# The end of a two-layer graph network: one row tile's root moved to GpSimd, four tiles' roots in one batch, and the last stores grouped otherwise

## The chip, the cores and the metric

The kernel runs on one core of one Trainium2 chip. The core has TensorE for matmuls, VectorE (DVE in the profile), ScalarE (ACT) and GpSimd (POOL) for everything elementwise, SyncE (SP), which here only issues DMAs, and 16 DMA engines. The metric is the time of one execution in microseconds (us) on the device, as the median of several runs.

## The reference

Sixteen graphs of 1024 nodes with 256 features each, and a 0/1 adjacency matrix for each. Two layers follow one another; each adds a message to the features and normalises every row.

```python
def _layernorm(x, axis=-1, eps=1e-5):
    m = jnp.mean(x, axis=axis, keepdims=True)
    v = jnp.var(x, axis=axis, keepdims=True)
    return (x - m) / jnp.sqrt(v + eps)

# layer 0: e0 = leaky(einsum('bid,bjd->bij', h * a0, h)); a0..a3 belong to adj == 1..4
alpha = sigmoid(where(adj == 1, e0, -max))          # adj is 0 or 1 in the data
x = _layernorm(x + einsum('bij,bjd->bid', alpha, h) + bias)

# layer 1
Hh = einsum('bni,io->bno', h, W)
s, d = Hh @ a_src, Hh @ a_dst
e = where(adj != 0, exp(-leaky_relu(s[:, :, None] + d[:, None, :], 0.2)), 0)
x = _layernorm(x + elu(einsum('bnm,bmo->bno', e, Hh) / rowsum(e)))
```

All the change happens in the last line, for the last graph: the quotient, the elu (which is `max(v, 0) + min(exp(v), 1) - 1`), the sum with the features, and the normalisation of each row, which needs the row's mean and the reciprocal root of its variance.

## The kernel before, in words

The main path (`one_kind_pass`) assumes that the adjacency holds only zeros and ones and checks that on the way; at the very end each engine reads a flag (`n_bad`), and a slow general path (`general_pass`) runs if the assumption failed. It does not fail on these data, so the timed execution takes the other branch, which holds only the last store (`y_last`).

The graphs go through in a software pipeline: while graph `b` is in layer 0, graph `b - 1` is in layer 1, and graph `b - 2` gets its last scalings and stores. A row tile is 128 nodes; a graph has eight. The order of all work is written out by hand: each engine works through its own instructions in the order in which the program issues them, and waits for others through semaphores. An instruction that waits holds up everything behind it on the same engine.

The last graph (`last`, index 15) has no next graph to run beside. Its layer 1 ends the kernel, and only this end is changed:

- TensorE sums tiles 0 to 3 together (`first`), then tiles 4, 5 and 6 one by one (`multiply1`), then tile 7 (`end`) in two halves of columns (`multiply_halves`): first columns 128 to 255 with the row sum, then columns 0 to 127. Each sum lies in a PSUM accumulator `acc`.
- For each tile, `elu` (lines 684 to 694) takes the reciprocal of the row sum on VectorE (`rinv`), then the relu and the exponential of the scaled sum on ScalarE (`h`, L693, and `y`, L694). For tile 6, VectorE makes `h` (L690, L691).
- `add` (L699, L706) joins them on VectorE, and `stats` (L326, L328) takes the mean and variance of the rows: `bn_stats` into `st`, then `bn_aggr` into `mv`. For tile 6 the aggregation is left for later.
- `center` turns the variances of a batch of tiles into `r` (the reciprocal root) and `mr` (minus mean times `r`) on GpSimd: L336 adds epsilon, L357 raises to the power of -0.5, L360 to L363 refine that by a Newton step, L373 and L374 make `mr`. Before the change it is called for tiles 0 to 2 at `t == 4`, and for tiles 3 to 5 at `t == 5`.
- `scale1` (L379) applies `r` and `mr` to a tile on ScalarE; `store` (L721) sends tiles out, from SP's queue or, with `nc.scalar`, from ScalarE's.
- At `t == 5` each engine reads the flag (L1064): ScalarE, SP and VectorE on their way, GpSimd behind its batch of roots. ScalarE then scales the last two tiles of graph 14, which SP stores, and then tiles 0 to 2 of graph 15.
- `end_half` (L1037 to L1043) does for each half of tile 7 what `elu`, `add` and `bn_stats` do for a whole tile. In the first half ScalarE makes the relu (L1037); in the second VectorE does (L1039). The exponential is ScalarE's in both (L1040).
- `root` takes the aggregation on VectorE (L960) and the square root on ScalarE (L962), which needs another activation table, so a table load stands ahead of it. `invert_roots` (L967 to L972) takes the reciprocal and a Newton step on VectorE, for tiles 6 and 7 together, two columns wide. Two VectorE instructions (L1089) then scale tiles 6 and 7 in `y_last`, and SP stores both (L1437).

Tiles 0 to 5 live in one buffer `y`, tiles 6 and 7 (`N_LAST = 2`) in `y_last`, which outlives the pass because the branch stores it.

Of the kernel before, what the change touches and what calls it, by code (L numbers as in the profile page):

```python
# [9 lines left out]
F32 = mybir.dt.float32  # L10
# [3 lines left out]
AF = mybir.ActivationFunctionType  # L14
ALU = mybir.AluOpType
# [3 lines left out]
P = 128  # L19
# [4 lines left out]
EPS = 1e-5  # L24
LOW = 1.0e-14
CHECKS = 4
N_LAST = 2


@with_exitstack  # L30
def one_kind_pass(
# [33 lines left out]
    nc = tc.nc  # L65
    B, N, D = x.shape
    NT = N // P
    ND = D // P
    HT = HALF // P
    assert ND == 2 and NT == 8 and HT == 4 and N_LAST == 2  # L70

    TINY = 1.0e-36
    N_BUSY = 7
    const = ctx.enter_context(tc.tile_pool(name="const", bufs=1))
# [81 lines left out]
    eps = const.tile([P, 1], F32, tag="eps", name="eps")  # L156
# [167 lines left out]
    def stats(y, mv, what):  # L324
        st = small.tile([P, nc.vector.BN_STATS_DIM], F32, tag="st", name=f"st_{what}")
        nc.vector.bn_stats(st, y)  # L326
        if mv is not None:
            nc.vector.bn_aggr(mv, st)  # L328
        return st

    def rstd(mv, what, add_eps=EPS, unit=1.0):

        n_t = mv.shape[1]
        ve = small.tile([P, NT], F32, tag="ve", name=f"ve_{what}")[:, 0:n_t]
        if unit == 1.0:
            nc.gpsimd.tensor_scalar(ve, mv[:, :, 1], add_eps, None, ALU.add)  # L336
        else:
            nc.gpsimd.tensor_scalar(ve, mv[:, :, 1], unit * unit * unit, add_eps, ALU.mult, ALU.add)  # L338
        return root_of(ve, what)
# [28 lines left out]
    def center(mv, what, add_eps=EPS, unit=1.0):  # L368

        r = rstd(mv, what, add_eps, unit)  # L370
        n = mv.shape[1]
        mr = small.tile([P, NT], F32, tag="mr", name=f"mr_{what}")[:, 0:n]
        nc.gpsimd.tensor_tensor(mr, mv[:, :, 0], r, ALU.mult)  # L373
        nc.gpsimd.tensor_scalar(mr, mr, -unit, None, ALU.mult)  # L374
        r_all[what] = r
        return [(r[:, t : t + 1], mr[:, t : t + 1]) for t in range(n)]

    def scale(y, r, mr):
        nc.scalar.activation(y, y, AF.Identity, bias=mr, scale=r)  # L379
# [265 lines left out]
    hs, ys, y_of, mv1s, r1s = {}, {}, {}, {}, {}  # L645
# [10 lines left out]
    def new_y(b):  # L656

        if True:
# [3 lines left out]
            else:  # L662
                y = one.tile([P, NT - N_LAST, D], F32, tag="xT", name=f"y_{b}")
                ys[b] = [y[:, m, :] for m in range(NT - N_LAST)]
                ys[b] += [y_last[:, m, :] for m in range(N_LAST)]
            y_of[b] = y
# [11 lines left out]
    def elu(b, t, acc, rinv=None):  # L678

        if t == 0:  # L680
            new_y(b)
        if rinv is None:
            rinv = small.tile([P, 1], F32, tag="rinv", name=f"rinv_{b}_{t}")
            nc.vector.tensor_scalar(rinv, acc[:, D : D + 1], TINY, None, ALU.max)  # L684
            nc.vector.reciprocal(rinv, rinv)
        hs[b, t] = two.tile([P, D], F32, tag="h", name=f"h_{b}_{t}")
        if (b, t) == (B - 1, NT - 2):

            h = hs[b, t]
            nc.vector.tensor_scalar(h, acc[:, 0:D], rinv, 0.0, ALU.mult, ALU.max)  # L690
            nc.vector.scalar_tensor_tensor(h, h, -1.0, x1s[b][:, t, :], ALU.add, ALU.add)  # L691
        else:
            nc.scalar.activation(hs[b, t], acc[:, 0:D], AF.Relu, scale=rinv)  # L693
        nc.scalar.activation(ys[b][t], acc[:, 0:D], AF.Exp, scale=rinv)  # L694

    def add(b, t, between=None):

        y = ys[b][t]
        nc.vector.scalar_tensor_tensor(y, y, 1.0, hs[b, t], ALU.min, ALU.add)  # L699
        if b < B - 1:  # L700
            nc.vector.scalar_tensor_tensor(
                y, y, -1.0, x1s[b][:, t, :], ALU.add, ALU.add, accum_out=mv1s[b][:, t, 0:1]
            )
            return None
        if (b, t) != (B - 1, NT - 2):
            nc.vector.scalar_tensor_tensor(y, y, -1.0, x1s[b][:, t, :], ALU.add, ALU.add)  # L706
        if between:
            between()

        full = (b, t) == (B - 1, NT - 2)  # L710
        return stats(y, None if full else mv1s[b][:, t, :], f"1_{b}_{t}")

    def deviation1(b, t):
        deviation(ys[b][t], mv1s[b][:, t, :])
# [1 line left out]
    def scale1(b, t):  # L716
        scale(ys[b][t], *r1s[b][t])

    def store(b, t0, n, queue=nc.sync):
        rows = out[b].rearrange("(t p) d -> p t d", p=P)  # L720
        queue.dma_start(rows[:, ds(t0, n), :], y_of[b][:, ds(t0, n), :])  # L721
# [59 lines left out]
    for b in range(1, B):  # L781
        prev, done = b - 1, b - 2
        last = b == B - 1
# [124 lines left out]
        for t in range(NT):  # L908
# [30 lines left out]
            if last and t in (4, 6):  # L939
                t0 = (t - 4) // 2 * HT  # L940
# [14 lines left out]
    last, done = B - 1, B - 2  # L955
    r1s[last] = []

    def root(t, st):

        nc.vector.bn_aggr(mv1s[last][:, t, :], st)  # L960
        r = roots_sb[:, t - (NT - 2) : t - (NT - 2) + 1]
        nc.scalar.activation(r, mv1s[last][:, t, 1:2], AF.Sqrt, bias=eps)  # L962

    def invert_roots():

        v, r = mv1s[last][:, NT - 2 :, 1], roots_sb
        nc.vector.reciprocal(r, r)  # L967

        n = const.tile([P, 2], F32, tag="newton", name="newton")
        nc.vector.scalar_tensor_tensor(n, v, EPS, r, ALU.add, ALU.mult)  # L970
        nc.vector.scalar_tensor_tensor(n, n, -0.5, r, ALU.mult, ALU.mult)
        nc.vector.scalar_tensor_tensor(r, n, 1.5, r, ALU.add, ALU.mult)  # L972
        return r

    roots_sb = const.tile([P, 2], F32, tag="root", name="root")
    n_first = 4
    first = [acc1(last, t, *((ps_e, "e") if t < 3 else (ps_t, "t"))) for t in range(n_first)]
    for m in range(NT):
# [23 lines left out]
    def multiply1(t):  # L1002
        accs.append(acc1(last, t, ps_acc, "acc"))
        for m in range(NT):
            sum1(last, t, accs[t], m)


    end = NT - 1
    half_cols = (slice(P, D), slice(0, P))

    def multiply_halves():
        for c, cols in enumerate((slice(P, D + 1), half_cols[1])):
            acc = acc1(last, end, *((ps_e, "e") if c else (ps_acc, "acc")))
            halves.append(acc[:, 0 : cols.stop - cols.start])
            for m in range(NT):
                nc.tensor.matmul(
                    halves[c],
                    lhsT=es[last][:, m, ts(end, P)],
                    rhs=Hs[last][m][:, cols],
                    start=(m == 0),  # L1020
                    stop=(m == NT - 1),
                )
# [22 lines left out]
    for t in range(end):  # L1045
        if n_first - 1 <= t < end - 1:
            multiply1(t + 1)
        if t == 5:
            multiply_halves()
        if t == 4:  # L1050
            total = ps_t.tile([P, HT, P], F32, tag="t", name="total")[0:1, 0, 0:1]
            nc.tensor.matmul(total, lhsT=any_bad, rhs=ones, start=True, stop=True)
        elu(last, t, accs[t])
        if 1 <= t < 6:
            add(last, t - 1)
        if t == 5:
            nc.vector.tensor_copy(flag, total)
            add(last, t)
        if t == 6:
            st_full = add(last, t, invert)  # L1060
        if t in (4, 5):
            r1s[last] += center(mv1s[last][:, ds(3 * t - 12, 3), :], f"1_{last}_{t}")
        if t == 5:
            n_bad = nc.values_load(  # L1064
                flag, min_val=0, max_val=P, skip_runtime_bounds_check_because="a number of partitions"
            )
        for q in range(2 * t - 4, 2 * t - 2) if 2 <= t < 6 else []:
            scale1(done, q)
            if q in (3, 7):
                store(done, q - 3, HT)  # L1070
        if t == 5:
            for q in range(3):
                scale1(last, q)
            store(last, 0, 3)
    h_end = two.tile([P, D], F32, tag="h", name="h_end")
    st_end = two.tile([P, 2, nc.vector.BN_STATS_DIM], F32, tag="low", name="st_end")
    end_half(0)
    scale1(last, 3)
    scale1(last, 4)
    store(last, 3, 2)  # L1080
    end_half(1)
    root(end, st_end)
    root(end - 1, st_full)
    r = invert_roots()
    scale1(last, 5)
    store(last, 5, 1, nc.scalar)
    for q in (6, 7):
        y = ys[last][q]
        nc.vector.tensor_scalar(  # L1089
            y, y, mv1s[last][:, q, 0:1], r[:, q - 6 : q - 5], ALU.subtract, ALU.mult  # L1090
        )
    return n_bad


# [310 lines left out]
def kernel(  # L1405
# [22 lines left out]
    with tc.tile_pool(name="flag", bufs=1) as flagp:  # L1428
        chk = flagp.tile([P, NCHK], F32, tag="chk", name="chk")
        fit = flagp.tile([P, B], F32, tag="fit", name="fit")  # L1430
        y_last = flagp.tile([P, N_LAST, x.shape[2]], F32, tag="y_last", name="y_last")
        n_bad = one_kind_pass(tc, x, adjT, a0, bias, W, a, out, chk, fit, y_last)
        with tc.If(n_bad > 0) as found:
            general_pass(tc, x, adjT, a0, a1, a2, a3, bias, W, a, out)
        with found.Else():
            rows = out[B - 1].rearrange("(t p) d -> p t d", p=P)
            nc.sync.dma_start(rows[:, ds(N // P - N_LAST, N_LAST), :], y_last)  # L1437

# [36 lines left out]
```

## Time and profile before

| what | value |
|---|---|
| median of 3 runs | 1218.76 us (1218.22 to 1219.0) |
| the profiled execution | 1218.96 us |
| its span | 1217.2 us |
| TensorE busy | 1206.9 us (99%) |
| granted TensorE clock, mean | 0.998 |
| VectorE, ScalarE, GpSimd busy | 82%, 70%, 32% |
| last matmul ends (modelled) | about 1209.3 us into the span |
| last store issued, landed | 1213.64, 1216.04 us into the span |

The span is the time from the first to the last recorded instruction; the run's own time is 1.76 us longer. Three kinds of view are read below. The page gives busy times of each engine over the whole span. The chain of waits follows the end back from the last instruction, each step with its start, its length, its engine, and the tile and line that it belongs to. The timeline lists single instructions of an engine: start, length, engine, line, operation, tile written and tiles read, shape, and in brackets how long the engine had been idle and what ended that. DMA issues are given with their size and the time from the issue to the landing of the data. A queue's own steps have a q behind the engine's name.

### The profile page before, as it was taken

How to read it: one execution, taken by the hardware profiler on the slowest of the kernel's cores; microseconds unless marked ns; L12 is line 12 of the kernel's file. 1: busy time of each engine (PE TensorE's matmuls, PEld its weight loads, DVE VectorE, ACT ScalarE, POOL GpSimd, SP SyncE). 2: the span in 40 equal slices, each digit the busy share in tenths (PEclk: the TensorE clock that was granted, in tenths of full speed). 3: DMA queues.
4: the chain of work that ended last, by engine and by line, in shares of the span. 5: the costliest groups of instructions: out<-in, count | busy, mean ns of one | idle time of the engine just before them, and what ended most of it. 6: DMA issues, size and time to landing. Idle time of an engine off the chain costs nothing.

```text
span 1217.2 us, 15868 instructions
## 1 busy us (share of the span) xinstructions
PE 1206.9 (99%) x4400; PEld 819.4 (67%) x4400; DVE 993.4 (82%) x1759; ACT 846.5 (70%) x2150; POOL 391.2 (32%) x730
## 2 busy tenths in 40 slices
PE   9999999999999999999999999999999999999997
PEld 6757657576575866758667585775757657576686
DVE  5698797887969789797897978879798796887957
ACT  4574867767687676867768677786776867577674
POOL 3320333404243142441414324143340433404243
PEclk9999999999999999999999999999999999999999
DMA  9568787797878878788787886877769787887512
GB/s 195 104 133 153 130 158 154 148 184 137 154 152 155 180 136 160 145 166 172 142 171 132 156 179 132 176 139 143 173 143 189 128 156 151 156 182 137 112 52 73
DMA packets 604600, 180.66 MB, mean 148 GB/s; under 512 B 482012, under 2 KB 586968, under 8 KB 604504
## 3 DMA queue, kind: packets, MB, share of 16 engines
q1 hardware_dynamic: 582800, 136.90, 56.0%
q0 software_dynamic: 21008, 42.01, 18.8%
q8 instruction: 37, 0.61, 0.2%
q10 hardware_dynamic: 696, 0.66, 0.2%
q14 instruction: 59, 0.48, 0.1%
HBM read 152.44 MB, written 60.62 MB: 175 GB/s over the span
## 4 chain that ended last, share of the span: by engine, by line
PE 96%; ACT 2%; DVE 1%; POOL 1%; DMA 0%; issue 0%; ACTq 0%; DVEq 0%; POOLq 0%
PE acc L648 36%; PE pe L254 20%; PE pH L582 9%; PE pQ L477 8%; PE pV L477 8%; PE pW L477 8%; PE pR L477 4%; PE acc L396 2%; ACT junk L130 0%; ACT y_kept L379 0%; DMA p_row<-row 0%; PE busy L149 0%; PE pal L313 0%; ACT x L379 0%; POOL ve L338 0%
## 5 line engine op out<-in xcount | busy, mean ns | idle before, releaser
L648 PE MATMUL acc<-H,e 128*128 128x257 f32 x2032 | 445.6, 380 | 0.6 <-DVE e L643 0.6
L648 PEld LDWEIGHTS acc<-H,e 128*128 128x128 f32 x2032 | 384.8, 190 | 64.8 <-issue 7.2
L254 PE MATMUL pe<-xa,xT 128*128 128x384 f32 (+1 forms) x720 | 249.5, 486 | 0.2 <-DVE xa L235 0.2
L254 PEld LDWEIGHTS pe<-xa,xT 128*128 128x128 f32 x720 | 132.8, 190 | 90.0 <-issue 50.7
L284 POOL TENSOR_TENSOR al<-ident,al 128x128 f32<-128x128 f32 x128 | 103.7, 818 | 198.6 <-DVE al L270 198.5
L643 DVE SCALAR_TENSOR_TENSOR e<-p,pq_kept,adj 128x1024 f32<-128x1024 f32 (+1 forms) x136 | 159.2, 1224 | 0.0
L455 DVE TENSOR_TENSOR al<-al 128x1024 f32<-128x1024 f32 (+2 forms) x105 | 144.9, 1380 | 11.7 <-POOL al L284 4.5
L264 DVE TENSOR_TENSOR tb<-tb,low 128x512 f32<-128x512 f32 (+1 forms) x192 | 104.7, 551 | 39.8 <-ACT low L263 39.7
L262 ACT ACTIVATE tb<-pe 128x512 f32<-128x512 f32 (+1 forms) x192 | 93.8, 489 | 59.4 <-PE pe L254 57.7
L130 ACT ACTIVATE junk<-adj,minus 128x2048 bf16<-128x2048 bf16 x64 | 127.3, 1990 | 0.0
L582 PE MATMUL pH<-Wx,yT 128*128 128x258 f32 x480 | 116.3, 380 | 0.0
L104 POOL CAST adj<-x 128x1 bf16<-128x1 f32 x15 | 3.2, 212 | 348.9 <-DMA x<-y_rows 298.4
L582 PEld LDWEIGHTS pH<-Wx,yT 128*128 128x128 f32 x480 | 91.2, 190 | 31.1 <-issue 13.4
L477 PE MATMUL pV<-al,S 128*128 128x512 f32 x240 | 107.9, 592 | 0.0
L477 PE MATMUL pW<-al,x 128*128 128x512 f32 x240 | 107.9, 592 | 0.0
L477 PE MATMUL pQ<-al,x 128*128 128x512 f32 x240 | 107.9, 592 | 0.0
L270 DVE SCALAR_TENSOR_TENSOR al<-tb,adj 128x512 f32<-128x512 f32 (+7 forms) x132 | 97.4, 739 | 4.5
L305 DVE SCALAR_TENSOR_TENSOR al<-al,adj 128x512 f32<-128x512 f32 (+3 forms) x150 | 81.6, 564 | 18.6 <-DMA al<-mir 18.1
L263 ACT ACTIVATE low<-pe 128x512 f32<-128x512 f32 (+1 forms) x192 | 94.1, 490 | 1.2 <-DVE tb L264 1.2
L379 ACT ACTIVATE y_kept<-y_kept,mr,r 128x256 f32<-128x256 f32 x120 | 64.9, 588 | 42.9 <-POOL mr L374 41.7
L674 ACT ACTIVATE sums<-acc,tiny 128x1 f32<-128x1 f32 x45 | 11.7, 261 | 111.0 <-PE acc L648 111.0
L684 DVE TENSOR_SCALAR rinv<-acc 128x1 f32<-128x1 f32 x82 | 12.8, 157 | 89.9 <-PE acc L648 89.8
(152 smaller groups left out, 1681.7 us busy)
## 6 DMA issues: line engine op xcount, KB each, us to landing
adj<-in_adjT POOLq DMA_DIRECT2D x30, 1024.0 KB, 8.4
x<-in_x SPq DMA_DIRECT2D x15, 1024.0 KB
y_rows<-Z SPq DMA_DIRECT2D x240, 64.0 KB, 2.0
x<-y_rows SPq DMA_DIRECT2D x30, 512.0 KB, 4.3
out<-y_kept SPq DMA_DIRECT2D x30, 512.0 KB, 3.0
xT<-in_x SPq DMA_DIRECT2D x112, 128.0 KB, 4.0
p<-p_row POOLq DMA_DIRECT2D x15, 512.0 KB, 4.2
mir<-tb SPq DMA_DIRECT2D x60, 112.0 KB, 3.0
```

Of the source, the lines that this page charges most:

```text
L130: nc.scalar.activation(junk, rows, AF.Square, bias=minus1, scale=2.0, accum_out=chk[:, b * CHECKS + n : b * CHECKS + n + 1],)
L254: nc.tensor.matmul(pe[:, 0:w], lhsT=xTs[b][:, c, ts(jt, P)], rhs=xas[b][:, c, ds(jt * P + o, w)], start=(c == 0), stop=(c == ND - 1),)
L262: nc.scalar.activation(tb[:, ds(o, w)], pe[:, 0:w], AF.Tanh, scale=0.5)
L263: nc.scalar.activation(low[:, 0:w], pe[:, 0:w], AF.Tanh, scale=0.5 * SLOPE)
L264: nc.vector.tensor_tensor(tb[:, ds(o, w)], tb[:, ds(o, w)], low[:, 0:w], ALU.max)
L270: nc.vector.scalar_tensor_tensor(als[b][:, jt, c0:c1], tbs[b, jt][:, c0 - jt * P : c1 - jt * P], 1.0, adjs[b, jt // HT][:, jt % HT, c0:c1] ...
L284: nc.gpsimd.tensor_tensor(diag, ident2, diag, ALU.add)
L455: nc.vector.tensor_tensor(out_, in0, in1, ALU.subtract)
L477: nc.tensor.matmul(banks[bank], lhsT=lhs[:, jt, :], rhs=rhs[:, jt, :], start=first and jt == 0, stop=jt == HT - 1, skip_group_check=True,)
L582: nc.tensor.matmul(pt, lhsT=x1Ts[b][:, c, ts(t, P)], rhs=Wx[:, c, :], start=(c == 0), stop=(c == ND - 1),)
L643: nc.vector.scalar_tensor_tensor(e, p_bcs[b][:, cols], q, rows, ALU.mult, ALU.min)
L648: nc.tensor.matmul(acc, lhsT=es[b][:, m, ts(t, P)], rhs=Hs[b][m], start=(m == 0), stop=(m == NT - 1),)
```

## The change

Tile 6 leaves `y_last` for the buffer `y` (`N_LAST = 1`). Its aggregation follows its statistics at once, and its root comes from `center` on GpSimd, as for tiles 0 to 5; ScalarE scales it and stores it together with tile 5. The square root on ScalarE, the Newton step and the scaling on VectorE are left for tile 7 alone. The batches of `center` become tiles 0 to 3 (called at `t == 4`), 4 and 5 (at `t == 5`) and 6 (at `t == 6`). ScalarE's scaling of tile 3 moves from between the two halves of tile 7 to ahead of the first; that of tile 4 stays between them. SP stores tiles 0 to 3 in one DMA and tile 4 in another, where it stored 0 to 2 and 3 and 4; ScalarE's queue stores 5 and 6, where it stored 5; the last store holds tile 7 alone.

```diff
-N_LAST = 2
+N_LAST = 1
...
-        full = (b, t) == (B - 1, NT - 2)
-        return stats(y, None if full else mv1s[b][:, t, :], f"1_{b}_{t}")
+        return stats(y, mv1s[b][:, t, :], f"1_{b}_{t}")
...
-    def root(t, st):
-
-        nc.vector.bn_aggr(mv1s[last][:, t, :], st)
-        r = roots_sb[:, t - (NT - 2) : t - (NT - 2) + 1]
-        nc.scalar.activation(r, mv1s[last][:, t, 1:2], AF.Sqrt, bias=eps)
-
-    def invert_roots():
-
-        v, r = mv1s[last][:, NT - 2 :, 1], roots_sb
+    def root():
+
+        mv = mv1s[last][:, NT - 1, :]
+        nc.vector.bn_aggr(mv, st_end)
+        v, r = mv[:, 1:2], const.tile([P, 1], F32, tag="root", name="root")
+        nc.scalar.activation(r, v, AF.Sqrt, bias=eps)
         nc.vector.reciprocal(r, r)
 
-        n = const.tile([P, 2], F32, tag="newton", name="newton")
+        n = const.tile([P, 1], F32, tag="newton", name="newton")
         nc.vector.scalar_tensor_tensor(n, v, EPS, r, ALU.add, ALU.mult)
         nc.vector.scalar_tensor_tensor(n, n, -0.5, r, ALU.mult, ALU.mult)
         nc.vector.scalar_tensor_tensor(r, n, 1.5, r, ALU.add, ALU.mult)
         return r
 
-    roots_sb = const.tile([P, 2], F32, tag="root", name="root")
...
         if t == 6:
-            st_full = add(last, t, invert)
-        if t in (4, 5):
-            r1s[last] += center(mv1s[last][:, ds(3 * t - 12, 3), :], f"1_{last}_{t}")
+            add(last, t, invert)
+        for t0, n in {4: [(0, 4)], 5: [(4, 2)], 6: [(6, 1)]}.get(t, []):
+            r1s[last] += center(mv1s[last][:, ds(t0, n), :], f"1_{last}_{t0}")
...
             for q in range(3):
                 scale1(last, q)
-            store(last, 0, 3)
+    scale1(last, 3)
+    store(last, 0, HT)
     h_end = two.tile([P, D], F32, tag="h", name="h_end")
     st_end = two.tile([P, 2, nc.vector.BN_STATS_DIM], F32, tag="low", name="st_end")
     end_half(0)
-    scale1(last, 3)
     scale1(last, 4)
-    store(last, 3, 2)
+    store(last, 4, 1)
     end_half(1)
-    root(end, st_end)
-    root(end - 1, st_full)
-    r = invert_roots()
+    r = root()
     scale1(last, 5)
-    store(last, 5, 1, nc.scalar)
-    for q in (6, 7):
-        y = ys[last][q]
-        nc.vector.tensor_scalar(
-            y, y, mv1s[last][:, q, 0:1], r[:, q - 6 : q - 5], ALU.subtract, ALU.mult
-        )
+    scale1(last, 6)
+    store(last, 5, 2, nc.scalar)
+    y = ys[last][end]
+    nc.vector.tensor_scalar(y, y, mv1s[last][:, end, 0:1], r, ALU.subtract, ALU.mult)
```

More of the change, by code (lines that the diff above doesn't have):

```diff
@@ L69, in one_kind_pass @@
     HT = HALF // P
-    assert ND == 2 and NT == 8 and HT == 4 and N_LAST == 2
+    assert ND == 2 and NT == 8 and HT == 4 and N_LAST == 1
     TINY = 1.0e-36
```

## The prediction

> **What bounds the kernel now.** I read the page first, for the engine that fills the span; then the chain of waits over the last 14 us, since the diff touches only the end of the last graph; then ScalarE's and GpSimd's rows in that stretch, and the DMA issues. All times are us from the start of the span of the one profiled execution.
>
> The page says that TensorE fills the kernel:
>
> ```profile
> span 1217.2 us, 15868 instructions
> PE 1206.9 (99%) x4400; PEld 819.4 (67%) x4400; DVE 993.4 (82%) x1759; ACT 846.5 (70%) x2150; POOL 391.2 (32%) x730
> ```
>
> None of the 1206.9 us of matmul is touched. TensorE's last matmul ends near 1209.3, so what the change can move is the 8 us after it, and the chain that leads there. The chain of waits, in order of time, there:
>
> ```profile
> 1205.52 1.18 ACT y L379 x3
> ...
> 1206.90 0.46 ACT y_last L694
> ...
> 1209.61 0.26 DVE h_end L1039
> 1209.87 0.02 issue
> 1209.89 0.37 ACT y_last L1040
> ...
> 1210.28 0.98 ACT L962
> ...
> 1211.57 0.49 ACT root L962 x2
> ...
> 1212.87 0.09 DVE y_last L1089
> 1212.96 0.24 issue
> 1213.20 0.41 DVE y_last L1089
> ```
>
> To be seen: ScalarE's three scalings hold up tile 6's exponential; the last exponential follows VectorE's L1039; a table load follows it; then two square roots, four small VectorE steps, two scalings of `y_last`, and the last store. ScalarE's own rows:
>
> ```profile
> 1208.19 0.37 ACT L1037 ACTIVATE h_end<-acc,rinv_end 128x128 f32<-128x128 f32 x1 [0.84 <-DVE rinv_end L1030]
> ...
> 1208.70 1.08 ACT L379 ACTIVATE y<-y,mr,r 128x256 f32<-128x256 f32 x2
> 1209.89 0.37 ACT L1040 ACTIVATE y_last<-acc,rinv_end 128x128 f32<-128x128 f32 x1
> 1210.28 1.28 ACT L962 ACT_TABLE_LOAD   x1
> ```
>
> ScalarE has a hole of 0.84 before L1037. GpSimd's first and last rows of a batch of four columns (an earlier one, of the same helper) and of the last batch of three:
>
> ```profile
> 1160.99 0.30 POOL L336 TENSOR_SCALAR ve<-mv 128x4 f32<-128x4 f32 x1 [24.51 <-DVE mv L328]
> ...
> 1164.06 0.41 POOL L374 TENSOR_SCALAR mr<-mr 128x4 f32<-128x4 f32 x1
> ```
>
> ```profile
> 1205.39 0.23 POOL L336 TENSOR_SCALAR ve<-mv 128x3 f32<-128x3 f32 x1 [2.15 <-DVE mv L328]
> ...
> 1208.22 0.25 POOL L374 TENSOR_SCALAR mr<-mr 128x3 f32<-128x3 f32 x1
> ```
>
> Four columns take 3.48, three take 3.08. The last stores, by size and time to landing:
>
> ```profile
> out<-y_kept SPq DMA_DIRECT2D x2, 512.0 KB, 3.0
> ...
> out<-y_last SPq DMA_DIRECT2D x1, 256.0 KB, 2.4
> out<-y ACTq DMA_DIRECT2D x1, 128.0 KB, 2.3
> ```
>
> The last store is issued at 1213.64, lands at 1216.04, and the span ends 1.16 later, in the closing branch and barrier, which stay.
>
> **The change, part by part.**
>
> *Square root.* One instead of two. The pair takes 0.49; ScalarE's other one-column instruction (L674, `sums`) takes 0.26. So reciprocal and what follows start 0.22 earlier (bounds 0 and 0.25). The three Newton steps work on one column instead of two: 0.16 to 0.17 each, the same as one-column rows of L684 and L685, so nothing.
>
> *Scaling of `y_last`.* One instead of two. The chain gives the first 0.09 + 0.24 before the second starts: 0.33 earlier. The last store is issued at 1213.64 - 0.22 - 0.33 = 1213.09.
>
> *Aggregation of tile 6* (0.13, at 1211.07) goes from behind the last one to right after its statistics, which end at 1208.40. Its old place lay under the table load (until 1211.56): no gain. In the new one VectorE is idle until 1208.59, waiting for `h_end`; it starts at about 1208.45 and the next instruction of VectorE follows such a row after 0.10. Cost 0; at most 0.07 if the full 0.18 of such rows stood in the way.
>
> *Scaling of tile 3* moves ahead of L1037, into the hole: from about 1207.35, 0.59 long, done by 1207.95, before 1208.19. Cost 0. Between the two exponentials one scaling is left, so ScalarE is free near 1209.3 instead of 1209.8. I put the gain at 0: the exponential starts 0.04 after the end of L1039 (1209.52 + 0.33 = 1209.85), which reads the same accumulator, but 0.11 after the scalings, while ScalarE's rows elsewhere start before the one ahead has ended. What released it was VectorE, and L1039 itself stands behind VectorE's statistics of the first half. So the exponential stays at 1209.89 and the table load at 1210.28 to 1211.56.
>
> The Trainium skill, "PSUM — Partial Sum Buffer", section "PSUM bank collisions raise a hardware error", speaks against a gain here: reads of one bank by ScalarE and VectorE must not overlap, so they are put one after the other. The rows agree, with 0.04 between them. By that rule the term is 0; without it the exponential could start near 1209.4, and the sum would be larger by about 0.47, as worked out under the first rival.
>
> *Roots of tiles 0 to 3 in one batch.* It must wait for tile 3's aggregation, at 1201.69, where the batch of three began at 1200.08. With the lag of 0.09 seen there it starts at 1201.78, and by the rows of four columns (3.48, and 3.33 from 1165.48) ends at 1205.1 to 1205.3. ScalarE wants it at 1205.42, behind the last graph's scalings: hidden, with 0.15 to 0.3 to spare. If that cover goes, everything behind ScalarE's three scalings is late by the same amount: tile 6's exponential, the first half of tile 7, the whole chain. Bounds: 0, and 1.9 by the 5.52 that eight columns took from 1187.08, beside a VectorE busy with wide operands. I take 0, by the rows of equal size.
>
> *Roots of tiles 4 and 5* start at 1205.39 as before, with two columns instead of three: 2.6 to 3.1, done by 1208.5. Scaling 4 wants them at 1208.70. Cost 0.
>
> *Root of tile 6 on GpSimd*: eight more instructions, behind GpSimd's read of the flag (0.78, at 1208.2 now). It starts at 1208.8 to 1209.3. No row has one column; the power step takes 2.05, 1.1, 0.89 for eight, four, three, so about 0.45 for one, and a batch some 2.65 (bounds 2.2 and 3.16, the batch of three). Done at 1211.0 to 1212.4, around 1211.6. Scaling 6 wants it after the square root and scaling 5, at 1211.57 + 0.20 + 0.50 = 1212.27. Cost 0, at most 0.2, and that on ScalarE's store alone.
>
> *Stores.* SP's first store waits for scaling 3 and goes out at about 1207.95 with 512 KB instead of 1207.02 with 384 KB; the second at about 1209.35 with 128 KB. By the 3.0 of 512 KB both have landed before 1212. SP has only the last store behind them. ScalarE's store grows to 256 KB and goes out after scaling 6, at 1212.27 + 0.59 + 0.03 = 1212.89 (now 1212.57). The last shrinks to 128 KB at 1213.09. Alone they would land at 1212.89 + 2.4 = 1215.29 and 1213.09 + 2.3 = 1215.39. But now they fly together, where in the trace ScalarE's 128 KB had moved (1213.45 to 1213.95) before the last store's 256 KB began (1214.5 to 1215.4). Lower bound: no interference, 1215.39. Upper bound: the small one moves wholly behind the large one: ScalarE's data starts 0.9 after issue, at 1213.8, takes 0.9 to 1.0, then 0.5, then 0.6 to 0.9 until landing, up to 1216.15. Between them, 384 KB as one store, by the rows of 256 and 512 KB, take 2.7: 1215.59 from the first issue, 1215.79 from the second. I take 1215.65.
>
> The Trainium skill, "DMA: Bandwidth & Descriptors", section "Issuing engines are not separate DMA queues", says that stores issued by different engines run on the same 16 DMA engines and interleave. Taken at its word the full gain at the issue does not reach the landing; two separate paths would give 1215.39. No row here has two such small stores at once.
>
> *Sum.* Landing 1216.04 to 1215.65: -0.39, or -0.55 at the issue with 0.16 given back by the stores. The profiled execution took 1218.96 around its span of 1217.2, so 1218.57; it lay 0.20 above the median of the three runs, so as a median 1218.76 - 0.39 = 1218.37, say 1218.4. Bounds of this case alone: -0.65 to +0.1.
>
> **The rivals.**
>
> *The last exponential is released by ScalarE.* Then it starts near 1209.4, the table load ends near 1211.1, and the square root waits for the aggregation, whose chain gets 0.09 shorter and ends at 1211.1: 0.47 more, in all -0.9, or 1217.9. Against it: the 0.04 above.
>
> *Nothing reaches the end.* ScalarE's store, twice as large and issued later, becomes the last to land, or the two disturb each other fully: landing 1215.95 to 1216.15, so 1218.7 to 1218.9. For it: 384 KB in flight in the last 2.5 us instead of 256.
>
> *Slower: GpSimd's third batch is late.* ScalarE's store waits for scaling 6, and its landing is 0.05 + 0.59 + 0.03 + 2.4 = 3.07 after that batch. It passes 1216.04 once the batch ends after 1212.97, which is 3.7 to 4.2 after its start. At the 5.52 of eight columns it ends at 1214.3 to 1214.8: +1.3 to +1.8, or 1220.1 to 1220.6. Against it: eight columns are the far end, and batches of three beside a working VectorE took 3.08 and 3.16.
>
> *The change does not do what it says*: the order of instructions on each engine shows one root, one `y_last` scaling and the new batches, so this would be a difference elsewhere, in 1200 us that nothing touches.
>
> **How the numbers follow.** Likeliest case 0.62; exponential earlier 0.08; nothing reaches the end 0.18; third batch late 0.09; anything else 0.03. The three runs of before lie 0.78 apart, so I add 0.4 on either side: from 1217.8 to 1217.4 below, and above from the second rival's 1218.9, past it into part of the third, to 1219.5. About 0.2% (2.4 us) is what a measurement of this kernel can tell from no change, and every worked-out case lies within it: same 0.95, faster 0.02, slower 0.03, from the last case and from the slower rival with the first batch late as well.
>
> **What the profile after would show.** One square root and a `y_last` scaling that starts about 0.55 earlier (right); the last exponential still right behind VectorE's read of the same accumulator, and the table load unmoved (right), or both 0.4 earlier (first rival). ScalarE's three scalings at 1205.4 without a wait for GpSimd. The third GpSimd batch done before 1212.3. ScalarE's store issued at 1212.9 and the last at 1213.1, landing between 1215.4 and 1215.8. The forecast is wrong if GpSimd's batches end later than ScalarE asks for them, or if the two stores together take longer than one of 384 KB.

## The result, and the profile after

The changed kernel takes 1220.43 us, the median of 22 runs, against 1218.54 for the kernel before in 22 runs beside them: a ratio of 1.0014, with a 95% interval of 1.0008 to 1.0021. That is 1.7 us more, with 1.0 to 2.6 as its bounds. A second set of 11 runs gave 1.0014 again (1.0005 to 1.0023). The forecast was 0.4 us less, in a range up to 1219.5.

The profiled execution of the changed kernel has a shorter span than that of the kernel before:

```profile
span 1216.9 us, 15876 instructions
PE 1206.0 (99%) x4400; PEld 819.4 (67%) x4400; DVE 993.8 (82%) x1758; ACT 846.7 (70%) x2150; POOL 392.9 (32%) x738
```

The difference lies in the 1200 us ahead, which the change does not touch and which vary from run to run. Over the twelve profiles of this study (all kernels share that part) the last exponential of tile 7 started anywhere between 1208.22 and 1211.79 us; here at 1208.22, in the kernel before at 1209.89. So all that follows is told from the start of that exponential, which I call zero. From zero to the end of the span it is 7.27 us before and 8.67 after: 1.40 longer, which lies within the 1.0 to 2.6 of the timed runs.

The chain of waits after, the same stretch as was shown of before (start, length, engine, tile, line):

```profile
1203.84 1.20 ACT y L379 x3
...
1205.23 0.46 ACT y L694
...
1207.93 0.26 DVE h_end L1034
...
1208.22 0.37 ACT y_last L1035
...
1208.60 1.28 ACT L962
...
1209.89 0.30 ACT root L962
...
1211.00 0.41 DVE y_last L1082
```

One square root and one scaling of `y_last`; the scaling starts 2.78 after zero, where the second of the two started at 3.31 before. ScalarE's rows:

```profile
1207.03 0.60 ACT L379 ACTIVATE y<-y,mr,r 128x256 f32<-128x256 f32 x1
1208.22 0.37 ACT L1035 ACTIVATE y_last<-acc,rinv_end 128x128 f32<-128x128 f32 x1 [0.59 <-DVE h_end L1034]
1208.60 1.28 ACT L962 ACT_TABLE_LOAD   x1
1209.89 0.29 ACT L962 ACTIVATE root<-mv,eps 128x1 f32<-128x1 f32 x1
1210.10 1.08 ACT L379 ACTIVATE y<-y,mr,r 128x256 f32<-128x256 f32 x2
```

ScalarE now stands idle for 0.59 ahead of the exponential and is released by VectorE's read of the accumulator; scalings 5 and 6 follow the root without a wait for GpSimd. GpSimd's three batches, first and last rows:

```profile
1200.13 0.23 POOL L336 TENSOR_SCALAR ve<-mv 128x4 f32<-128x4 f32 x1 [9.09 <-DVE mv L328]
...
1203.38 0.24 POOL L374 TENSOR_SCALAR mr<-mr 128x4 f32<-128x4 f32 x1
...
1207.15 0.23 POOL L336 TENSOR_SCALAR ve<-mv 128x1 f32<-128x1 f32 x1 [0.35 <-ACT y_last L1035]
...
1209.59 0.24 POOL L374 TENSOR_SCALAR mr<-mr 128x1 f32<-128x1 f32 x1
```

The batch of one column takes 2.68 and is done at 1209.83, before ScalarE's scaling 6 at about 1210.6. The DMA issues of the end:

```profile
out<-y ACTq DMA_DIRECT2D x1, 256.0 KB, 2.9
out<-y SPq DMA_DIRECT2D x1, 128.0 KB, 3.7
out<-y_last SPq DMA_DIRECT2D x1, 128.0 KB, 2.9
```

The last store is issued at 1211.44, 3.23 after zero (3.75 before), and lands at 6.15 (6.12 before): what was gained at the issue is gone at the landing. The rest of the loss comes later still, in the part that I had called "the closing branch and barrier, which stay". It is seen in the instructions of the queues, by source line: the branch on the flag (L1433 before, L1424 after) and the end of the kernel (L1471, L1462). The columns are operation, count, shortest, median and longest duration in ns, and first and last start. GpSimd and SP in the kernel before, at the branch:

```profile
L1433 POOLq EVENT_SEMAPHORE  x5: 17/43/43, 1211.7 to 1212.0; - x5
L1433 POOLq COMPARE_BRANCH  x1: 45/45/45, 1209.0 to 1209.0; - x1
...
L1433 POOLq INC_SWDGE_SEM  x1: 836/836/836, 1212.1 to 1212.1; - x1
```

and at the end:

```profile
L1471 POOLq DRAIN  x3: 46/107/2682, 1213.0 to 1216.9; - x3
L1471 SPq DRAIN  x3: 7/7/7, 1216.3 to 1216.6; - x3
```

After, at the branch:

```profile
L1424 POOLq EVENT_SEMAPHORE  x5: 17/43/43, 1212.1 to 1212.4; - x5
...
L1424 POOLq COMPARE_BRANCH  x1: 45/45/45, 1209.5 to 1209.5; - x1
...
L1424 POOLq INC_SWDGE_SEM  x1: 832/832/832, 1212.5 to 1212.5; - x1
```

and at the end:

```profile
L1462 POOLq DRAIN  x3: 46/107/2682, 1213.4 to 1216.6; - x3
L1462 SPq DRAIN  x3: 7/7/7, 1215.1 to 1216.3; - x3
```

To be seen: GpSimd has a way out of its own. It branches, its next instruction comes 2.5 to 2.7 us later, then an `INC_SWDGE_SEM` of 0.83, then a `DRAIN` of 2.68; with some small waits between, 6.5 to 6.6 us from branch to the end of the drain. Before, the branch stood at 0.88 ahead of zero, the drain ended at 5.76, and SP, which waits for the landing of all stores, was through at 6.45: GpSimd had 0.69 to spare. After, the third batch holds the branch back to 1.32 behind zero, the drain ends at 7.83, and SP has been through since 6.92. The engines meet at a last barrier, 0.8 ahead of the end, and wait for GpSimd.

### The profile page after: what moved, and what is told of

The parts are those of the page before. It is cut to its first block, busy times and chain, and to the rows that moved or that the text cites. A ratio compares the mean times of both kernels' runs of the same rounds, so it can differ in the third digit from the quotient of the medians.

```text
span 1216.9 us, 15876 instructions
## 1 busy us (share of the span) xinstructions
PE 1206.0 (99%) x4400; PEld 819.4 (67%) x4400; DVE 993.8 (82%) x1758; ACT 846.7 (70%) x2150; POOL 392.9 (32%) x738
## 4 chain that ended last, share of the span: by engine, by line
PE 98%; DVE 1%; ACT 1%; issue 0%; ACTq 0%; DVEq 0%
PE acc L648 36%; PE pe L254 20%; PE pH L582 9%; PE pV L477 8%; PE pW L477 8%; PE pQ L477 8%; PE pR L477 4%; PE acc L396 2%; PE busy L149 0%; PE pal L313 0%; PE prow L610 0%; ACT L962 0%; ACT y L379 0%; DVE y L699 0%; ACT y_kept L379 0%
## 5 line engine op out<-in xcount | busy, mean ns | idle before, releaser
L284 POOL TENSOR_TENSOR al<-ident,al 128x128 f32<-128x128 f32 x128 | 110.7, 873 | 199.3 <-DVE al L270 199.1
```

The lines of the kernel that those rows point to most:

```text
L284: nc.gpsimd.tensor_tensor(diag, ident2, diag, ALU.add)
```

## The experiments

Theory G: GpSimd's way out ends last, because tile 6's root puts 2.7 us of work in front of it. The rivals: S, the two last stores in flight together are the loss; M, the loss lies in the 1200 us ahead; R, the regrouped batches and SP's stores cost something themselves. The table holds all runs, in us from zero, by the trace of one profile each (GpSimd: end of its drain; SP: through its closing waits), and the times against the kernel before on the same chip.

| kernel | last store issued, landed | SP through | GpSimd through | end | ratio to before (95%) |
|---|---|---|---|---|---|
| before | 3.75, 6.12 | 6.45 | 5.76 | 7.27 | 1 |
| changed | 3.23, 6.15 | 6.92 | 7.83 | 8.67 | 1.0014 (1.0008 to 1.0021) |
| changed, again | 3.23, 5.95 | 6.94 | 7.83 | 8.67 | 1.0014 (1.0005 to 1.0023) |
| changed, no third batch | 3.23, 6.21 | 6.96 | 6.37 | 7.78 | 1.0005 (0.9996 to 1.0014) |
| before, GpSimd + 10 instructions | 3.74, 6.78 | 7.04 | 8.21 | 9.04 | 1.0012 (1.0003 to 1.0021) |
| before, GpSimd + 2 instructions | 3.75, 6.24 | 6.55 | 6.27 | 7.37 | 0.9996 (0.9987 to 1.0005) |
| changed, root of tile 6 back | 3.75, 6.31 | 6.63 | 6.37 | 7.45 | 1.0000 (0.9991 to 1.0009) |
| changed, no branch | 3.23, 5.55 | 5.82 | 4.32 | 6.93 | 0.9996 (0.9987 to 1.0005) |
| before, no branch | 3.75, 5.88 | 6.14 | 1.6 | 6.96 | 0.9996 (0.9987 to 1.0005) |
| before, one root, no Newton | 2.97, 5.84 | 6.11 | 5.77 | 6.93 | 0.9995 (0.9986 to 1.0004) |
| changed, no third batch, early store | 3.23, 5.80 | 6.32 | 6.37 | 7.21 | one run, 1219.25 against 1220.79 |
| one root, two stores | 3.56, 6.19 | 6.51 | 6.30 | 7.33 | 1.0002 (0.9993 to 1.0011) |

**The third batch taken away.**

```diff
-        for t0, n in {4: [(0, 4)], 5: [(4, 2)], 6: [(6, 1)]}.get(t, []):
+        for t0, n in {4: [(0, 4)], 5: [(4, 2)]}.get(t, []):
...
-    scale1(last, 6)
+    scale(ys[last][6], *r1s[last][5])
```

> The changed kernel without GpSimd's third batch: scaling 6 uses tile 5's root, so tile 6 of the last graph comes out wrongly scaled; every store, scaling and VectorE step stays. Theory G (GpSimd's way out of the kernel, some 6.5 us from its last instruction to the closing barrier, now ends last): in the changed kernel's profile GpSimd reaches the barrier at 1216.05 and SP, the next, at 1215.13, so without the batch the kernel is 0.9 us shorter than the changed one, about 1.0 longer than before, and SP arrives last. Theory S (the last two stores in flight together are the whole loss): nothing changes, about 1.9 longer than before. Theory M (chance in the 1200 us ahead): as theory S.

Measured: 7.78 to the end, 0.89 less than the changed kernel, and 1.0005 in time. Its queue rows at the branch, then at the end:

```profile
L1424 POOLq EVENT_SEMAPHORE  x5: 17/43/43, 1214.2 to 1214.5; - x5
...
L1424 POOLq COMPARE_BRANCH  x1: 45/45/45, 1210.6 to 1210.6; - x1
```

```profile
L1462 POOLq DRAIN  x3: 46/107/2682, 1215.5 to 1219.3; - x3
L1462 SPq DRAIN  x3: 7/7/7, 1218.7 to 1219.0; - x3
```

GpSimd branches at 1.1 ahead of zero (which is 1211.79 here) and its drain, 2.68 from 1215.5, ends before SP's at 1218.7. Nothing else changed, so the batch costs the 0.9. It is the traces that show this, where GpSimd's marks in the changed kernel repeat to 0.01; the intervals of the timed runs overlap. What stays, 0.5 against the kernel before where 1.0 was expected, is SP's. Theory G holds for the larger part; the rest is late landings and SP's waits behind them.

**Work for GpSimd that nobody waits for**, in the kernel before, behind its reading of the flag:

```diff
+    idle = const.tile([P, 1], F32, tag="idle", name="idle")
+    nc.gpsimd.memset(idle, 1.0)
+    for _ in range(9):
+        nc.gpsimd.tensor_tensor(idle, idle, idle, ALU.mult)
     h_end = two.tile([P, D], F32, tag="h", name="h_end")
```

> The kernel before, with one memset and nine dependent one-column multiplications on GpSimd behind its reading of the flag, which nobody waits for; some 2.6 us of work by the rows of 0.27 each. Theory G: GpSimd had 0.69 us to spare (its drain ends at 1215.65, SP is through at 1216.34), so the kernel gets 1.7 to 2.0 us longer. Theory S and theory M: no change.

The same with `range(1)`:

> The kernel before, with one memset and one multiplication on GpSimd behind the reading of the flag, some 0.4 to 0.5 us. Theory G: inside the 0.69 us that GpSimd had to spare, so no change (within 0.2 us). If any work on GpSimd at the end costs its own time: 0.4 to 0.5 us longer.

Measured: with ten instructions the drain ends at 8.21 and the end comes at 9.04, 1.77 later than in the kernel before, as theory G had it; the time is 1.0012. With two, GpSimd is through at 6.27, still ahead of SP, and the end moves by 0.1. The rows of the long one at the end of the kernel:

```profile
L1475 POOLq DRAIN  x3: 46/107/2682, 1217.1 to 1220.4; - x3
L1475 SPq DRAIN  x3: 7/7/7, 1218.6 to 1220.1; - x3
```

Here GpSimd's drain starts at 1217.1 and lasts until 1219.8, and SP has been through since 1218.6. The stores are issued, and the scalings start, as in the kernel before. One thing does differ: the last store took 3.04 to land, against 2.37, and with that SP alone would have made 0.59 of the 1.77; the other 1.16 is GpSimd beyond SP. Only work on GpSimd was added, so such work is enough to make the loss, and most of it by the wait for GpSimd itself; whether the later landing comes of it too is not shown. Theories S and M fall as the main cause.

**Tile 6's root back** on ScalarE and VectorE, the rest as changed:

```diff
-        if t in (4, 5):
-            r1s[last] += center(mv1s[last][:, ds(3 * t - 12, 3), :], f"1_{last}_{t}")
+        for t0, n in {4: [(0, 4)], 5: [(4, 2)]}.get(t, []):
+            r1s[last] += center(mv1s[last][:, ds(t0, n), :], f"1_{last}_{t0}")
...
-            store(last, 0, 3)
+    scale1(last, 3)
+    store(last, 0, HT)
...
-    scale1(last, 3)
     scale1(last, 4)
-    store(last, 3, 2)
+    store(last, 4, 1)
```

(against the kernel before)

> The changed kernel with tile 6's aggregation, square root, Newton step, scaling and store as before; the batches of tiles 0 to 3 and 4 and 5, the early scaling of tile 3 and SP's stores of four tiles and one tile as changed. Theory G: as before within 0.3 us, GpSimd's batch of two ends a little sooner than that of three. Theory R (the regrouped batches or SP's stores cost something themselves): still longer than before by 0.5 us or more.

Measured: 7.45 and 1.0000. Theory R falls by the trace, with 0.18 more where it asked for 0.5 (the timed interval leaves 1.1 us either way): batches, early scaling and SP's stores cost nothing that can be told. One detail was wrong: GpSimd is not through sooner but later (6.37 against 5.76), because 3.5 us lie between its branch and its next instruction here, against 2.7. The length of this hole differs from kernel to kernel, 2.5 to 3.5. The DMA records have something that goes with it: on the queue that the views call `instruction`, a packet of 8 KB starts 1.7 us after GpSimd's branch in the four profiles with a hole of 3.5, 1.2 after it in the one with 3.0, and 1.0 after it in the five with 2.5 to 2.7. What holds that packet up was not tried.

**Without the branch.** The general path and the branch are left out. The source still reads the flag, but the traces have no load of it, only a wait on a semaphore at that line, so the loads are gone too; in the changed kernel the last batch of roots ends where it did with them (1.62 against 1.61 after zero):

```diff
-        with tc.If(n_bad > 0) as found:
-            general_pass(tc, x, adjT, a0, a1, a2, a3, bias, W, a, out)
-        with found.Else():
-            rows = out[B - 1].rearrange("(t p) d -> p t d", p=P)
-            nc.sync.dma_start(rows[:, ds(N // P - N_LAST, N_LAST), :], y_last)
+        rows = out[B - 1].rearrange("(t p) d -> p t d", p=P)
+        nc.sync.dma_start(rows[:, ds(N // P - N_LAST, N_LAST), :], y_last)
```

> The changed kernel without the general path and without the branch around it; the engines still read the flag and then run straight on, so the check has no consequence here. Theory G, in the form that most of GpSimd's way out is the jump (2.5 us between its branch and its next instruction) and the drain (2.7): without the jump GpSimd arrives about 2.5 earlier and SP ends the kernel; from the last exponential to the end 7.7 us as in the run without the third batch (7.78) instead of 8.67, so 0.9 to 1.0 shorter than the changed kernel and 0.4 longer than before. If the drain alone matters and the jump overlaps it: as the changed kernel, 8.6.

> The same with the kernel before. Theory G: SP ended it and GpSimd had 0.69 to spare, so the jumps cost nothing there: 7.2 to 7.3 from the last exponential to the end as before, within 0.2 us. If the jumps bound the kernel before as well: 1 to 3 us shorter.

Measured: 6.93 and 6.96 to the end, 0.9996 both. The two kernels end alike once no engine has a branch to take; how much of this is GpSimd's branch alone, this pair of runs does not tell. The rows of the changed one at the end:

```profile
L1459 POOLq DRAIN  x3: 46/113/2992, 1212.4 to 1217.4; - x3
...
L1459 SPq DRAIN  x3: 7/7/7, 1216.8 to 1217.1; - x3
```

GpSimd's drain starts at 1212.4, 1.3 after zero (1211.05), at the end of the last batch, where with the branch it started at 5.15; it lasts 2.99 and ends long before SP's 1216.8. The `INC_SWDGE_SEM` is gone with the branch too. For the changed kernel the gain is larger than I had put it, since the stores land sooner as well: 2.2 and 2.3 after their issue, against 2.9 and 2.9, and SP is through 0.27 after the last landing instead of 0.77. Of that, 0.3 is lost again behind the barrier, in one step of GpSimd that takes 0.33 there and 0.04 elsewhere. In the kernel before the same shows, 2.13 against 2.37, and its end comes 0.31 sooner, a little outside what was expected. So with the branch, stores take longer to land. The trace has another difference: from 2 us ahead of zero to the end, nine packets on the queues called `instruction` in each of the ten profiles with the branch, and one and none in the two without. So instructions are fetched there while the stores are in flight; that this gets in their way is the likely reason, argued and not shown.

**A shorter chain** in the kernel before:

```diff
-        r = roots_sb[:, t - (NT - 2) : t - (NT - 2) + 1]
-        nc.scalar.activation(r, mv1s[last][:, t, 1:2], AF.Sqrt, bias=eps)
...
+        nc.scalar.activation(r, v, AF.Sqrt, bias=eps)
         nc.vector.reciprocal(r, r)
-
-        n = const.tile([P, 2], F32, tag="newton", name="newton")
-        nc.vector.scalar_tensor_tensor(n, v, EPS, r, ALU.add, ALU.mult)
-        nc.vector.scalar_tensor_tensor(n, n, -0.5, r, ALU.mult, ALU.mult)
-        nc.vector.scalar_tensor_tensor(r, n, 1.5, r, ALU.add, ALU.mult)
         return r
...
+    root(end - 1, st_full)
     root(end, st_end)
-    root(end - 1, st_full)
     r = invert_roots()
```

> The kernel before with one square root over two columns, and without the Newton step behind it, which leaves the roots of tiles 6 and 7 less exact. The last store is issued 0.22 + 0.59 = 0.8 earlier. Theory G: the gain is cut off where the next engine arrives, ScalarE or GpSimd, 0.6 to 0.7 ahead of SP in the profile before: 0.6 shorter, so 6.6 to 6.7 from the last exponential to the end. Without such a bound: 0.8 shorter.

Measured: the store is issued 0.78 sooner, but lands 2.87 after that, and 0.34 is left at the end, where 0.6 was expected. GpSimd (5.77) and ScalarE (5.93) were through before SP (6.11), so it was not their bound that cut the gain off but the landing. A miss in its reason, if not in its direction.

**The changed kernel again:**

> The changed kernel once more, for a second profile and an interval on the same chip as the others. Theory G: GpSimd is again the last to the barrier, its branch some 1.3 us after the start of the last exponential, 8.6 to 8.7 from there to the end. If the first profile was chance: SP last, or another length.

Measured: every mark of GpSimd's way out at the same place to 0.01 (branch 1.32, drain 5.15 to 7.83), and the same end, 8.67.

**The rest of the loss.** The run without the third batch, and without scaling 6; scaling 5 beside 4:

```diff
     scale1(last, 4)
+    scale1(last, 5)
     store(last, 4, 1)
...
-    scale1(last, 5)
-    scale(ys[last][6], *r1s[last][5])
```

> As the run without the third batch, and also without the scaling of tile 6 (tile 6 of the last graph is stored unscaled); the scaling of tile 5 stands beside that of tile 4. So ScalarE's store of 256 KB goes out right after the square root, about 2.0 us after the start of the last exponential instead of 3.0, and has landed before SP goes through its list of semaphores. In the run without the third batch SP was through at 6.96, 0.75 after the last landing, because it had to wait for ScalarE's store first and then go through some 14 further waits of 0.065. Theory W (the order of SP's closing waits makes a late store on ScalarE's queue dear): SP through 0.3 after the last landing, as in the kernel before, so at about 6.4 to 6.5. Theory S (only that the two stores share the DMA engines): the last store lands 2.3 to 2.4 after its issue instead of 3.0, and SP is through 0.75 after that. Both can be true.

Measured, in one run: ScalarE's store went out under the table load, at 1.36, and had landed at 4.08. The last store then landed 2.57 after its issue instead of 2.98, and SP was through 0.52 after that instead of 0.75 (0.29 of it one long step of SP). Both parts moved the way they were expected to, by 0.4 and 0.2; 7.21 to the end is the kernel before's 7.27. GpSimd, through at 6.37, came last here by 0.05. One run does not settle their sizes, since the landing alone varies by 0.2 between two profiles of one kernel.

**A version from these runs**: tile 6's root with tile 7's in one two-column square root, tiles 4 and 5 scaled between the exponentials and stored early by SP, nothing stored by ScalarE.

```diff
-        r = roots_sb[:, t - (NT - 2) : t - (NT - 2) + 1]
-        nc.scalar.activation(r, mv1s[last][:, t, 1:2], AF.Sqrt, bias=eps)
...
+        nc.scalar.activation(r, v, AF.Sqrt, bias=eps)
...
     scale1(last, 4)
-    store(last, 4, 1)
+    scale1(last, 5)
+    store(last, 4, 2)
     end_half(1)
-    root(end, st_end)
     root(end - 1, st_full)
+    root(end, st_end)
     r = invert_roots()
-    scale1(last, 5)
-    store(last, 5, 1, nc.scalar)
```

(against the run with tile 6's root back)

> A version drawn from the runs: tile 6's root stays with tile 7's, but as one square root over two columns (0.22 saved at the last store's issue, as the changed kernel kept); GpSimd's batches are tiles 0 to 3 and 4 and 5; scalings 4 and 5 stand between the two exponentials, so tiles 4 and 5 go out in one store from SP's queue 3 us before the last one, and ScalarE stores nothing. Theory G: the last store is issued 3.5 after the start of the last exponential, lands 2.4 later, SP is through 0.3 after that, at 6.2 to 6.3; GpSimd arrives at 5.8 to 6.4 and may end last; 7.0 to 7.2 to the end against 7.27 in the kernel before, 8.67 in the changed one. In time: the changed kernel's 1.4 to 1.9 us are gone, and against the kernel before 0.1 to 0.3 us, less than can be told. If something else than GpSimd's way out and the late stores cost the changed kernel its time: longer than before.

Measured: 1.0002, 7.33 to the end. The changed kernel's loss is gone. The 0.2 saved at the issue is there (3.56), but the store took 2.63 to land and the end is no sooner than before. No version of this study is faster than the kernel before by more than can be told.

## Why the prediction was wrong

*What held.* The last store's issue: 3.20 after zero was forecast (1213.09), 3.23 measured. ScalarE's store: 3.00 and 2.99. Batch of four inside its margin (done at 1203.62, wanted at 1203.75), batch of one 2.68 where 2.65 had been put. Scaling 6 did not wait. The exponential stayed behind VectorE's read of its accumulator, which was the point of the rule on PSUM banks that was weighed: the trace has ScalarE idle for 0.59 there, so the first rival is out.

*What was mis-sized: the stores.* The landing was taken at 1215.65, 5.76 after zero; it came at 6.15, near the upper bound of 1216.15 (6.26). The gain of 0.39 was counted from a landing at 1216.04, which stands at 1216.01 in the trace of before. Both stores took 2.9. SP's closing added 0.44, which had no place in the sum: it checks the semaphores of the stores in a fixed order, and ScalarE's store, now landing late (5.86, where it was 5.02), comes ahead of some 14 further waits of 0.065, so that SP was through 0.77 after the last landing instead of 0.33. The early store bore both out in direction, in one run. The Trainium skill's rule that was weighed ("DMA: Bandwidth & Descriptors", section "Issuing engines are not separate DMA queues": stores from different engines share the same DMA engines) pointed to the dearer end of the range, and the packet records agree: the last store's first packet of data started 1.42 after its issue, when 85% of the packets of ScalarE's store had started, against 0.88 in the kernel before and 0.85 with the early store. So its data began 4.65 after zero, where it was 4.63: the gain at the issue was gone already there, and without the branch it is the same (4.66). The rest of the late landing is the end of the data: the last packet ended at 5.73 with the branch and 5.20 without. SP's store of tile 4 was late as well: it was to land before 1212 and landed 3.14 after zero, 1213.03 on that clock; nothing waited for it.

*What failed.* Two sentences: that the span ends "in the closing branch and barrier, which stay", and that the root of tile 6 on GpSimd costs "0, at most 0.2, and that on ScalarE's store alone". I had looked for who waits for the batch's result, found scaling 6 and the spare time before it, and stopped. But the closing barrier waits for the engine itself. The rival that ended on the slower side had the right engine and the wrong wait: its deciding point was a batch that ends after 1212.97, and the batch ended, on that clock, at 1211.50, well inside, and cost 0.91 all the same. That this rival's 1220.1 to 1220.6 holds the measured 1220.43 is luck. The table of the marks gives the sum that should have stood there: 0.03 at the landing, 0.44 in SP's closing, 0.91 for GpSimd beyond SP, 0.02 in the barrier, 1.40 in all.

*What could have been read.* Everything was in the profile of the kernel before: the queue rows of L1433 and L1471 shown above give GpSimd's branch at 1209.0, the hole of 2.7, and the drain of 2.68 that ends 0.69 ahead of SP. With the third batch done around 1211.6, as the prediction had it, the branch comes 2.6 later against 0.69 to spare: an estimate of 1.9 us longer from these rows, where 1.40 was measured. The page counts none of these as busy time, and its chain ends at the last instruction of an engine, so no row of the two views that I went by has them. The Trainium skill gives a reason for the hole, in "Runtime: NRT & Kernel Launch", section "Instruction fetch mechanics": instructions are fetched ahead in sequence, and a taken branch to a place outside what has been fetched has to wait for a DMA to bring it. The trace agrees: 2.5 to 3.5 us from GpSimd's branch to its next instruction, 3.1 and 3.4 for VectorE's and ScalarE's in the changed kernel, with instruction packets in that stretch, and neither without the branch. SP's next instruction comes 0.47 after its branch in both kernels; why it is spared is not shown.

*The bound of 0.2%.* The measured 0.14% lies within it, as 0.95 of the chance had it; the range did not hold the time, since each case in it was built on the same closing.

## What to carry to other kernels

At the end of a kernel each engine has to leave, not only to deliver: read from the queue rows how long each takes from its last instruction to the last barrier, and count work moved to an engine against that, even if its result comes in time. GpSimd's way out was 6.5 to 7.5 us here, a jump over the general path and a drain, against the 2.4 to 3.0 of a store's landing; VectorE and ScalarE have a jump of 2.5 to 3.5 but no such drain, so the last work belonged to one of them. And where a stretch ahead varies by more than the change can move, set both profiles to one mark close to the change and compare from there.

## What was not expected of the hardware

- GpSimd's last `DRAIN` took 2.682 us in every profile with the branch, whatever stood before it, and 2.91 and 2.99 without.
- From the end of the branch over the general path to the next instruction it took 2.5 to 3.5 us on GpSimd, 2.8 to 3.3 on VectorE, 2.5 to 3.5 on ScalarE, and 0.42 on SP.
- The landing of the last store took 2.37 to 3.04 after its issue in the kernels with the branch, for 128 and 256 KB alike, and 2.13 and 2.32 in those without.
- The reading of one flag took 0.46 us on SP, 0.47 on ScalarE, 0.54 on VectorE and 0.78 on GpSimd in the kernel before; in the changed kernel it took GpSimd 0.50.
